# A graph network layer stack: one graph's aggregation of messages moved into the next graph, and a transpose moved ahead of the distances

## The chip, the cores and the metric

The program runs on one core of one Trainium2 chip. The time is the device time of one execution in microseconds (us); the kernel before takes 2127.64 us (median of three runs, 2127.56 to 2128.44). The engines are named as the profile names them: PE (TensorE, matmuls) and PEld (its weight loads), DVE (VectorE), ACT (ScalarE), POOL (GpSimd), SP (SyncE, which only issues transfers here). Each engine works through its own queue in order. A letter q behind an engine (ACTq) is its sequencer, which issues transfers.

## What is computed

For 64 graphs of 256 nodes with 256 channels, in float32, two layers one after the other, each added to its input and normalized:

```python
# layer 0
deg = adj.sum(-1);  dis = deg ** -0.5
norm_adj = dis[:, :, None] * adj * dis[:, None, :]
x1 = layernorm(x + ((norm_adj + alpha * I) @ x) @ W.T + b)
# layer 1
x_conv = relu(bn2(conv17(relu(bn1(conv1(x1))))) + x1)    # along the nodes
s = x1 @ w_se.T + b_se
A = exp(-(sq[:, :, None] + sq[:, None, :] - 2 * s @ s.T)) * adj
msg = relu(x1 @ w_msg.T + b_msg)
x_nmp = A @ msg                                          # the aggregation
out = layernorm(x1 + gru([x_conv, x_nmp], x1))
```

The kernel does the convolution over 17 nodes by a Fourier transform over tiles of nodes, and the GRU's input as one matrix product with a Strassen scheme.

## The kernel before

The 64 graphs go through in four quarters of 16 (`Q`). For a quarter, first each graph's front part runs, layer 0 and what layer 1 can do before the convolution: `layer0` and `layer1` are Python generators, each cut by `yield` into pieces. `graphs` interleaves them: while layer 1 of graph g runs, layer 0 of graph g+2 runs in its gaps. Behind a quarter come the products of the convolution in the frequency domain (`products`, p_k in the profile), the transforms back (`complex_end` and others, many small DVE operations on the tile VM), and the gates (`gru`, p_g) of its graphs. The stages of different quarters overlap: the first 12 graphs of quarter 1 and the first 6 of quarters 2 and 3 (`AHEAD`) run while the quarter before is still in its products and transform; the filter weights (p_u) are made between the graphs of quarter 0.

`layer1` has seven pieces for a graph g:

- 0: x1 is transposed (`x1_transposed`: four PE transposes into p_x1T, and the copies of the two halves into `xn`, one by DVE (L430) and one by ACT (L431)), unless that was done ahead;
- 1: the first convolution and the three columns s (p_conv, L446), their copies by ACT into h and scols, and three small DVE operations (L454 to L457);
- 2: the messages (p_msg, L467, copied by ACT, L470);
- 3: the Fourier transform of h (p_dft, L482, copied by ACT, L487);
- 4: transposes of the columns (p_rows, L495), copied by ACT into dist_l (L497) and by DVE into dist_r (L499);
- 5: the distances (p_dist, L506), Exp by ACT into aT (L507), times the adjacency by DVE (L508);
- 6: the aggregation (p_nmp, L515), its copy by ACT into `xn` (L519) and the transfer of `xn` to memory (L520), issued by ACT.

In the 12 graphs of `ALONE` (16 to 27) x1 of the next graph is transposed at the start of piece 6.

`layer0` of graph g+2 has these parts: degrees by ACT (L356), transposes of adj on PE (p_adjT, L378), copied by ACT (L379), with the diagonal set by DVE (L381), and x scaled by ACT (L391); then p_hT (L399) and its copy by ACT (L404); then p_out (L409) and two DVE operations (L414); then the statistics of the normalization (DVE L325 to L327, a power on POOL, L328); then the normalization (DVE L331, ACT L333) and the transfer of x1.

`PLACES` says behind which piece of layer 1 a part of layer 0, or one of other work (weights, gates), is taken; `STATS` is the piece at which the statistics are taken, and `APPLIED` that at which the normalization of the layer 0 begun a graph earlier is run to its end:

```python
PLACES = (("other",), ("layer0",), (), (), ("layer0",), ("other", "layer0"), ())
STATS, APPLIED = len(PLACES) - 1, 2
```

The kernel's text does not fix each engine's order alone: a scheduler takes instructions by the order of the text and by when it reckons them ready, and hands out buffers from pools. `xn` has two buffers, `msg`, `aT` and `h` one, `adjT` three; the PSUM banks of the front part are a ring of four. `mark` names an operation behind which pieces of the transform's end are put (`paced`, with `RATES`).

Of the kernel before, what the change touches and what calls it, by code (L numbers as in the profile page):

```python
# [14 lines left out]
P = 128  # L15
# [11 lines left out]
def kernel(  # L27
# [27 lines left out]
    nc = tc.nc  # L55
# [4 lines left out]
    NCH = N // P  # L60
    DCH = D // P
# [20 lines left out]
    def bank(name):  # L82
        return ps.tile([P, 512], F32, tag="bank", name=name)
# [7 lines left out]
    def mark(op, gates=0):  # L91
        marks.append((op.ins, gates))
# [11 lines left out]
    def load(g):  # L104
        if g >= B:
            return
        ain[g] = loads.tile([P, NCH, N], F32, name="adj_t")
        nc.sync.dma_start(ain[g], adj[g].rearrange("(c p) m -> p c m", p=P))
        xin[g] = loads.tile([P, NCH, D], F32, name="x_t")
        nc.sync.dma_start(xin[g], x[g].rearrange("(c p) f -> p c f", p=P))  # L110
# [229 lines left out]
    xn_d = [dram.tile([P, 2 * DCH, N], F32, name=f"xn_d{g}") for g in range(B)]  # L340
    XN = {}
    ALONE = set()
# [80 lines left out]
    def x1_transposed(g):  # L423
        x1 = X1.pop(g)
        xn = XN[g] = work.tile([P, 2 * DCH, N], F32, name="xn")
        p = bank("p_x1T").rearrange("p (k n) -> p k n", k=DCH)
        for k in range(DCH):
            for c in range(NCH):
                nc.tensor.transpose(p[:, k, c * P : (c + 1) * P], x1[:, c, k * P : (k + 1) * P], ident)
        nc.vector.tensor_scalar(xn[:, 0], p[:, 0], others_only, unit, op0=ALU.mult, op1=ALU.add)  # L430
        nc.scalar.copy(xn[:, 2 * DCH - 1], p[:, 1])  # L431

    def layer1(g, place):

        if g not in XN:
            x1_transposed(g)
        xn, adjT = XN.pop(g), ADJT.pop(g)
        x1T = xn[:, 0 : 2 * DCH : 2 * DCH - 1]
        yield

        h = work.tile([P, NCH, D], F32, name="h", bufs=1)
        cols = scols.rearrange("p c (q r) -> p c q r", r=32)
        for c in range(NCH):
            p = bank("p_conv1")[:, : D + NSE]
            for k in range(DCH):
                nc.tensor.matmul(  # L446
                    p, x1T[:, k, c * P : (c + 1) * P], wc1[:, k, :], start=k == 0, stop=k == DCH - 1
                )
            nc.scalar.activation(h[:, c, :], p[:, :D], AF.Relu)
            nc.scalar.copy(cols[:, c, :, :NSE], p[:, D:].unsqueeze(1).to_broadcast([P, 4, NSE]))  # L450

        s3 = cols[:, :, 0, :NSE]
        sq3 = small.tile([P, NCH, NSE], F32, name="sq3")
        nc.vector.scalar_tensor_tensor(sq3, s3, -1.0, s3, op0=ALU.mult, op1=ALU.mult)  # L454
        nsq = small.tile([P, NCH], F32, name="nsq")
        nc.vector.tensor_reduce(nsq, sq3, AX.X, ALU.add)
        last = nc.vector.tensor_scalar(  # L457
            cols[:, :, 2:4, NSE], nsq.unsqueeze(2).to_broadcast([P, NCH, 2]), 0.5, None, op0=ALU.mult
        )
        mark(last)  # L460
        mark(last)
        yield
        msg = work.tile([P, NCH, D], F32, name="msg", bufs=1)
        p = bank("p_msg").rearrange("p (c d) -> p c d", c=NCH)
        for c in range(NCH):
            for k in range(DCH):
                nc.tensor.matmul(  # L467
                    p[:, c, :], x1T[:, k, c * P : (c + 1) * P], wmsg[:, k, :], start=k == 0, stop=k == DCH - 1
                )
        mark(nc.scalar.activation(msg, p, AF.Relu))  # L470
        yield


        mid = GT // 2
        if TILES[0] is not V:
            AWAY.append(place)
        for k in range(DCH):
            p = bank("p_dft")

            for c, t0, t1 in ((0, 0, mid + 1), (1, mid - 1, GT)):  # L480
                first = t0 + 1 - c * mid
                nc.tensor.matmul(  # L482
                    p[:, t0 * FL : t1 * FL], h[:, c, k * P : (k + 1) * P],
                    fwd[:, first : first + t1 - t0, :].rearrange("p t f -> p (t f)"),
                    start=c == 0, stop=True, skip_group_check=c == 1,
                )
            nc.scalar.copy(  # L487
                TILES[0][:, :, k, place * GT : (place + 1) * GT],
                p[:, : GT * FL].rearrange("p (t f) -> p f t", f=FL),
            )  # L490

        yield
        p = bank("p_rows")
        for c in range(NCH):
            nc.tensor.transpose(p[:, c * P : (c + 1) * P], scols[:, c, :], ident)  # L495
        dl = work.tile([64, N], F32, name="dist_l", bufs=1)
        nc.scalar.copy(dl, p[0:64, :N])  # L497
        dr = work.tile([64, N], F32, name="dist_r", bufs=1)
        nc.vector.tensor_copy(dr, p[64:P, :N])  # L499
        yield  # L500

        aT = work.tile([P, NCH, 2, P], F32, name="aT", bufs=1)
        for c in range(NCH):
            rows = slice(32 * c, 32 * c + 32)
            p = bank("p_dist")[:, :N]
            nc.tensor.matmul(p, dl[rows, c * P : (c + 1) * P], dr[rows, :], start=True, stop=True)  # L506
            nc.scalar.activation(aT[:, c].rearrange("p n q -> p (n q)"), p, AF.Exp, bias=nsq[:, c : c + 1], scale=2.0)  # L507
        mark(nc.vector.tensor_mul(aT, aT, adjT[:, :, 0:3:2, :]))  # L508
        yield
        if g in ALONE:  # L510
            x1_transposed(g + 1)
        p = bank("p_nmp").rearrange("p (k n) -> p k n", k=DCH)
        for k in range(DCH):
            for mc in range(NCH):
                nc.tensor.matmul(  # L515
                    p[:, k, :], msg[:, mc, k * P : (k + 1) * P], aT[:, mc].rearrange("p n q -> p (n q)"),
                    start=mc == 0, stop=mc == NCH - 1,
                )
        nc.scalar.copy(xn[:, 1 : 1 + DCH], p)  # L519
        nc.scalar.dma_start(xn_d[g], xn)  # L520
        yield

# [410 lines left out]
    def chain(*stages):  # L935
        for stage in stages:
            yield from stage
# [13 lines left out]
    def run(stage):  # L951
        for _ in stage:
            pass
# [14 lines left out]
            yield  # L968


    PLACES = (("other",), ("layer0",), (), (), ("layer0",), ("other", "layer0"), ())
    STATS, APPLIED = len(PLACES) - 1, 2
    ENDS = [iter(())]

    def graphs(first, part, others):


        for i in part:
            load(first + i + 3)
            given = {"layer0": layer0(first + i + 2) if first + i + 2 < B else iter(()), "other": others[i]}  # L980
            for piece, _ in enumerate(layer1(first + i, i)):
                if piece == APPLIED:
                    run(ENDS.pop())
                    ENDS.append(given["layer0"])
                elif piece == STATS:
                    next(given["layer0"], "end")
                yield
                for name in PLACES[piece]:
                    if next(given[name], "end") != "end":
                        yield  # L990
            yield from given["other"]

    with tc.tile_pool(name="setup", bufs=1) as setup:
        load_taps(setup, 0)
# [51 lines left out]
        others = [weights(setup, i, scale2) for i in range(NPARTS)]  # L1046
        others += [take(more_weights, i) for i in (1, 3, 2)]
        run(graphs(0, range(Q), others))
    ustream = ctx.enter_context(tc.tile_pool(name="ustream", bufs=6))

    def open_ahead(graphs):

        scope = ExitStack()
        pool = scope.enter_context(tc.tile_pool(name="ahead", bufs=1))
        return scope, graphs, pool.tile([P, FL, DCH, graphs * GT], F32, name="V2")
# [24 lines left out]
    def copies(V2):  # L1080

        waiting = list(AWAY)
        AWAY.clear()
        TILES[0] = V
        for i in waiting:
            nc.scalar.copy(V[:, :, :, i * GT : (i + 1) * GT], V2[:, :, :, i * GT : (i + 1) * GT])
            yield

    late = nothing()
    for q in range(NQ):  # L1090
        first = (q + 1) * Q
        more = q + 1 < NQ
        end = chain(complex_end(q), copies(V2) if more else iter(()))
# [99 lines left out]
```

## Time and profile before

| | |
|---|---|
| median of 3 runs | 2127.64 us (2127.56 to 2128.44) |
| the profiled execution | 2127.71 us, of which the span 2125.9 us |
| PE busy | 2006.1 us, 94% |
| PEld busy | 1443.2 us, 68% |
| DVE busy | 1474.1 us, 69% |
| ACT busy | 905.3 us, 43% |
| POOL busy | 666.8 us, 31% |
| granted PE clock, mean | 0.988 of full |

The profile is of one execution. Instructions are grouped by line of the kernel, engine, operation and tiles, written out<-in; "idle before" is the time for which the engine had nothing to run just before them, and the arrow names what ended it. A matmul in float32 shows as two records, so four matmuls of the text are eight in the profile. Matmuls are pipelined: their single durations overlap, so that eight records of 379 ns, started one after the other, take 1.73 us.

### The profile page before, as it was taken

The numbers are of one execution on the slowest core, as the hardware profiler recorded it, in microseconds if no ns is written. First come the engines' busy times: TensorE is split into PE (matmuls) and PEld (weight loads), VectorE is DVE, ScalarE is ACT, GpSimd is POOL, SyncE is SP. The second block draws the span as 40 slices with busy tenths as digits, with TensorE's granted clock in tenths as the row PEclk, the third lists the DMA queues.
The fourth block names the chain that finished last, engine by engine and source line by source line (L and its number), as shares of the span: only waits on it lengthen the run. The fifth ranks groups of instructions, "written<-read, shape, count | busy, mean of one in ns | idle before, by whom it ended". The sixth has DMA issues, their size and how long they took to land. (4 is left out here: it accounts for less than half of the span.)

```text
span 2125.9 us, 26260 instructions
## 1 busy us (share of the span) xinstructions
PE 2006.1 (94%) x8157; PEld 1443.2 (68%) x8157; DVE 1474.1 (69%) x3347; ACT 905.3 (43%) x2114; POOL 666.8 (31%) x672
## 2 busy tenths in 40 slices
PE   6999999888999999999999999999999999899997
PEld 5888788766667756667777666667777765555554
DVE  5555567775558788774556888875445889977776
ACT  4666643456432234555553123446554123233333
POOL 3445310121431243223321234323232123344443
PEclk9999999999999999999999999999999999999999
DMA  4766556433437645344335655334323754443331
GB/s 125 230 210 200 192 183 209 154 132 119 122 96 226 194 123 139 114 120 120 94 99 179 201 155 140 118 104 134 96 93 100 243 146 131 111 118 95 93 94 56
DMA packets 305289, 298.05 MB, mean 140 GB/s; under 512 B 84192, under 2 KB 283956, under 8 KB 305150
## 3 DMA queue, kind: packets, MB, share of 16 engines
q1 hardware_dynamic: 245198, 200.37, 32.1%
q10 hardware_dynamic: 44480, 67.39, 8.9%
q0 software_dynamic: 15472, 28.61, 6.0%
q8 instruction: 66, 1.08, 0.2%
q14 instruction: 73, 0.60, 0.1%
HBM read 193.19 MB, written 103.06 MB: 139 GB/s over the span
## 5 line engine op out<-in xcount | busy, mean ns | idle before, releaser
L856 PE MATMUL p_g<-wall,sums 128*128 128x384 f32 x1536 | 537.7, 489 | 11.6 <-DVE G L882 11.6
L856 PE MATMUL p_g<-wall,inputs 128*128 128x384 f32 x1152 | 409.4, 492 | 14.5 <-DVE G L874 14.1
L856 PEld LDWEIGHTS p_g<-wall,sums 128*128 128x128 f32 x1536 | 284.6, 191 | 200.3 <-issue 19.1
L856 PEld LDWEIGHTS p_g<-wall,inputs 128*128 128x128 f32 x1152 | 218.5, 192 | 167.5 <-DVE G L874 23.4
L838 POOL TENSOR_TENSOR sums<-inputs 128x384 f32<-128x384 f32 x128 | 139.9, 1093 | 343.2 <-PE p_g L856 296.9
L369 POOL TENSOR_TENSOR dis<-deg,neg_half 128x2 f32<-128x2 f32 x64 | 48.3, 754 | 475.7 <-DVE deg L367 468.6
L897 ACT ACTIVATE G<-G 128x512 f32<-128x512 f32 x128 | 80.7, 630 | 250.8 <-DVE G L884 148.6
L328 POOL TENSOR_TENSOR ln_rs<-ln_rs,neg_half 128x2 f32<-128x2 f32 x129 | 94.9, 736 | 275.1 <-DVE ln_rs L327 226.7
L541 PE MATMUL p_k<-u,VM 128*128 128x256 f32 x736 | 175.8, 381 | 4.1 <-DMA u<-ud 4.1
L541 PEld LDWEIGHTS p_k<-u,VM 128*128 128x128 f32 x736 | 139.4, 191 | 31.3 <-DMA u<-ud 3.9
L446 PE MATMUL p_conv<-wc,xn 128*128 128x259 f32 x512 | 130.4, 392 | 22.7 <-DVE xn L430 21.5
L399 PE MATMUL p_hT<-adjT,x 128*128 128x256 f32 x512 | 126.7, 391 | 15.6 <-ACT msg L470 8.2
L333 ACT ACTIVATE x_g<-x_g,ln_mr,ln_rs 128x256 f32<-128x256 f32 x128 | 70.0, 593 | 150.3 <-DVE ln_mr L331 148.3
L446 PEld LDWEIGHTS p_conv<-wc,xn 128*128 128x128 f32 x512 | 94.2, 191 | 53.1 <-DVE xn L430 31.1
L508 DVE TENSOR_TENSOR aT<-aT,adjT 128x512 f32<-128x512 f32 x64 | 44.8, 699 | 123.0 <-ACT aT L507 122.8
L409 PE MATMUL p_out<-w,hT 128*128 128x256 f32 x512 | 123.7, 384 | 3.4 <-ACT hT L404 3.0
L482 PE MATMUL p_dft<-fwd,h 128*128 128x240 f32 x512 | 117.4, 372 | 9.2 <-ACT scols L450 8.8
L515 PE MATMUL p_nmp<-aT,msg 128*128 128x256 f32 x512 | 122.6, 383 | 0.7 <-DVE aT L508 0.7
L467 PE MATMUL p_msg<-wmsg,xn 128*128 128x256 f32 x512 | 122.0, 381 | 0.0
L838 POOL TENSOR_TENSOR sums<-inputs,sums 128x384 f32<-128x384 f32 x64 | 70.2, 1097 | 161.3 <-PE p_g L856 160.6
L331 DVE SCALAR_TENSOR_TENSOR ln_mr<-ln_mv,ln_rs 128x2 f32<-128x2 f32 x129 | 47.3, 368 | 101.7 <-POOL ln_rs L328 101.7
L409 PEld LDWEIGHTS p_out<-w,hT 128*128 128x128 f32 x512 | 95.6, 190 | 29.9 <-ACT hT L404 9.9
(160 smaller groups left out, 3642.0 us busy)
## 6 DMA issues: line engine op xcount, KB each, us to landing
u<-ud SPq DMA_DIRECT2D x284, 256.0 KB
xn_d<-xn ACTq DMA_DIRECT2D x64, 512.0 KB
inputs<-xn_d SPq DMA_DIRECT2D x64, 512.0 KB
ud<-u_set POOLq DMA_DIRECT2D x39, 480.0 KB, 6.3
adj_t<-in_adj_dram SPq DMA_DIRECT2D x64, 256.0 KB
x_t<-in_x_dram SPq DMA_DIRECT2D x64, 256.0 KB
x_d<-x ACTq DMA_DIRECT2D x64, 256.0 KB
xc_d<-VM SPq DMA_DIRECT2D x64, 256.0 KB
```

The costliest lines, as they stand in the source:

```text
L328: nc.gpsimd.tensor_tensor(rs[:, : len(chunks)], rs[:, : len(chunks)], neg_half[:, : len(chunks)], op=ALU.pow)
L333: nc.scalar.activation(y[:, c, :], y[:, c, :], AF.Identity, bias=mr[:, c : c + 1], scale=rs[:, c : c + 1])
L399: nc.tensor.matmul(p[:, k, :], x1[:, mc, k * P : (k + 1) * P], adjT[:, mc, 1 - mc : 3 - mc, :].rearrange("p n q -> p (n q)"), start=mc == ...
L409: nc.tensor.matmul(p[:, c, :], hT[:, k, c * P : (c + 1) * P], w0[:, k, :], start=k == 0, stop=k == DCH - 1)
L446: nc.tensor.matmul(p, x1T[:, k, c * P : (c + 1) * P], wc1[:, k, :], start=k == 0, stop=k == DCH - 1)
L467: nc.tensor.matmul(p[:, c, :], x1T[:, k, c * P : (c + 1) * P], wmsg[:, k, :], start=k == 0, stop=k == DCH - 1)
L482: nc.tensor.matmul(p[:, t0 * FL : t1 * FL], h[:, c, k * P : (k + 1) * P], fwd[:, first : first + t1 - t0, :].rearrange("p t f -> p (t f)") ...
L515: nc.tensor.matmul(p[:, k, :], msg[:, mc, k * P : (k + 1) * P], aT[:, mc].rearrange("p n q -> p (n q)"), start=mc == 0, stop=mc == NCH - 1,)
L541: nc.tensor.matmul(p[:, j * D : (j + 1) * D], v[:, k, :], u[:, k, :], start=k == 0, stop=k == DCH - 1)
L838: nc.gpsimd.tensor_tensor(S[i], x, y, op=op)
L856: nc.tensor.matmul(p[:, : 3 * HD] if k == 0 else p[:, HD:], a[:, k], wall[:, b, k].rearrange("p t d -> p (t d)"), start=first and k == 0, ...
L897: nc.scalar.activation(rz, rz, AF.Tanh, scale=0.5)
```

## The change

The aggregation of a graph is taken out of its last piece. The graph only notes what is to be aggregated, in a list `PENDING`; a new function `aggregated` does it in the next graph, as a piece of its own between the adj transposes (which follow piece 1) and the messages. At the end of each run of `graphs` it is called once more for the last graph. The transposes of the next graph's x1, in the graphs of `ALONE`, go to the start of the distances' piece. The pieces are numbered anew: 0 and 1 as before, 2 the aggregation, 3 messages, 4 Fourier transform, 5 rows, 6 distances. The statistics of the layer 0 begun a graph earlier now run behind piece 1 instead of at the end of the graph before, and its normalization behind the messages, as before.

```diff
         mark(last)
         mark(last)
         yield
+        aggregated()
+        yield
         msg = work.tile([P, NCH, D], F32, name="msg", bufs=1)
...
         nc.vector.tensor_copy(dr, p[64:P, :N])
         yield
 
+        if g in ALONE:
+            x1_transposed(g + 1)
         aT = work.tile([P, NCH, 2, P], F32, name="aT", bufs=1)
...
         mark(nc.vector.tensor_mul(aT, aT, adjT[:, :, 0:3:2, :]))
-        yield
-        if g in ALONE:
-            x1_transposed(g + 1)
-        p = bank("p_nmp").rearrange("p (k n) -> p k n", k=DCH)
-        for k in range(DCH):
-            for mc in range(NCH):
-                nc.tensor.matmul(
-                    p[:, k, :], msg[:, mc, k * P : (k + 1) * P], aT[:, mc].rearrange("p n q -> p (n q)"),
-                    start=mc == 0, stop=mc == NCH - 1,
-                )
-        nc.scalar.copy(xn[:, 1 : 1 + DCH], p)
-        nc.scalar.dma_start(xn_d[g], xn)
-        yield
+        PENDING.append((g, xn, msg, aT))
+        yield
+
+    PENDING = []
+
+    def aggregated():
+
+        while PENDING:
+            g, xn, msg, aT = PENDING.pop()
+            p = bank("p_nmp").rearrange("p (k n) -> p k n", k=DCH)
+            for k in range(DCH):
+                for mc in range(NCH):
+                    nc.tensor.matmul(
+                        p[:, k, :], msg[:, mc, k * P : (k + 1) * P], aT[:, mc].rearrange("p n q -> p (n q)"),
+                        start=mc == 0, stop=mc == NCH - 1,
+                    )
+            nc.scalar.copy(xn[:, 1 : 1 + DCH], p)
+            nc.scalar.dma_start(xn_d[g], xn)
...
-    PLACES = (("other",), ("layer0",), (), (), ("layer0",), ("other", "layer0"), ())
-    STATS, APPLIED = len(PLACES) - 1, 2
+    PLACES = (("other",), ("layer0",), (), (), (), ("layer0",), ("other", "layer0"))
+    STATS, APPLIED = 1, 3
     ENDS = [iter(())]
...
             for piece, _ in enumerate(layer1(first + i, i)):
-                if piece == APPLIED:
-                    run(ENDS.pop())
-                    ENDS.append(given["layer0"])
-                elif piece == STATS:
-                    next(given["layer0"], "end")
+                if piece == STATS:
+                    next(ENDS[0], "end")
+                elif piece == APPLIED:
+                    run(ENDS[0])
+                    ENDS[0] = given["layer0"]
                 yield
...
             yield from given["other"]
+        aggregated()
```

## The prediction

> **What bounds the kernel now.** I read the page's head first, then busy times by stretch of the span, then the waits in the stretches that the change touches, and last the timeline of one graph.
>
> ```profile
> span 2125.9 us, 26260 instructions
> PE 2006.1 (94%) x8157; PEld 1443.2 (68%) x8157; DVE 1474.1 (69%) x3347; ACT 905.3 (43%) x2114; POOL 666.8 (31%) x672
> ```
>
> PE is the engine to watch. The next view cuts the span into stages (columns: window, length, busy time and instructions of PE, weight loads, DVE, ACT, POOL, then granted clock).
>
> ```profile
> 240.00:285.00 45.00, 41.01 (x193) 33.85 (x194) 24.42 (x74) 24.90 (x68) 11.24 (x13) 0.96 0.47 150
> ...
> 390.00:516.00 126.00, 109.73 (x536) 87.87 (x537) 95.99 (x273) 69.33 (x188) 24.26 (x26) 1.00 0.37 123
> 516.00:640.00 124.00, 111.00 (x421) 77.21 (x420) 61.48 (x138) 57.70 (x135) 43.58 (x46) 0.94 0.41 111
> ...
> 840.00:1140.00 300.00, 288.17 (x1251) 212.87 (x1250) 184.06 (x478) 159.25 (x400) 90.03 (x92) 1.00 0.36 108
> ...
> 1350.00:1640.00 290.00, 277.36 (x1190) 202.88 (x1189) 170.75 (x447) 149.22 (x374) 84.66 (x86) 0.99 0.34 105
> ```
>
> Graphs run in these windows, in 32-240 (graphs 0-12, filter weights between; PE busy 204.88 of 208) and in 285-390 (104.07 of 105). 640-840, 1140-1350 and all from 1640 on are transform products and gates, which the edit doesn't reorder. Those two full windows have no room. In the five shown PE is idle 4, 16, 13, 12 and 13 us. Who is waited for in 390-516 (sum, times, longest):
>
> ```profile
> DVE aT L508 <- ACT aT L507: 15.5, 8, 2.9
> ...
> DVE ln_mr L331 <- POOL ln_rs L328: 9.9, 9, 1.1
> PE p_conv L446 <- DVE xn L430: 9.6, 7, 3.1
> ```
>
> DVE's 95.99 busy and its waits of 15.5 and 9.9 make 121.4 of 126 us: there DVE, stuck in its own order, is the bound, and PE waits for it. In 840-1140 PE's waits are of another kind:
>
> ```profile
> PE p_hT L399 <- ACT msg L470: 4.5, 4, 2.2
> PE p_conv L446 <- DVE xn L430: 1.8, 3, 1.1
> PE p_rows L495 <- DVE ln_mv L326: 1.6, 1, 1.6
> PE p_rows L495 <- DVE scols L457: 1.3, 2, 0.9
> ```
>
> A row for p_dft behind scols adds 0.7. In 1350-1640 the same rows read 3.7, 1.8, 1.6, 1.3, and 2.0 for p_dft. Last, four rows of the timeline at one graph's end:
>
> ```profile
> 464.79 0.70 PE L506 MATMUL p_dist<-dist_r,dist_l 32*128 32x256 f32 x4
> ...
> 466.39 0.69 DVE L508 TENSOR_TENSOR aT<-aT,adjT 128x512 f32<-128x512 f32 x1 [2.59 <-ACT aT L507]
> ...
> 470.59 0.54 DVE L430 TENSOR_SCALAR xn<-p_x1T,others_only,ident 128x256 f32<-128x256 f32 x1
> ...
> 471.18 1.14 PE L446 MATMUL p_conv<-wc,xn 128*128 128x259 f32 x4 [1.49 <-DVE xn L430]
> ```
>
> PE had been through with the aggregation (p_nmp) for 1.5 us when conv could start, because DVE copied xn late.
>
> **The change part by part.** No instruction is added or removed: the same matmuls, copies and transfers in another order. Every term is an amount of waiting. I read the order from the built programs of both kernels.
>
> *Aggregation later.* Per graph 8 matmul records go from behind p_out to behind the next graph's adj transposes; they take 1.73 us (1414.07 to 1415.81 in the chain). Before, they hid little: in all but 12 graphs p_x1T came after them, so conv waited for xn's copy anyhow. After, 1.73 us more PE work stands between conv and msg, dft, rows and hT, the four that wait for ACT and DVE. ACT also gets the aggregation's copy (0.59) and the issue of xn_d (0.33) there, in front of msg's copy: for waits on ACT's queue the cover is 1.73 - 0.59 = 1.1 (the issue is the sequencer's and lets ACT's next operation start at once in the timeline). In the two long windows: dft 0.7 + 2.0, all single waits under 1.73, go; rows 2.9 + 2.9 go; p_nmp's own wait for aT, 0.3 + 0.4, goes; hT for msg, 8.2 in seven, loses 6.0 (two of 2.2 keep 1.1 each); conv 3.6 loses half, as a p_g group follows p_x1T in most graphs. That is 17.0. But in 840-940 DVE is 81% busy with the transform's end; there PE waits for DVE's work, not for a latency, and more cover doesn't shorten it. I take half: **-8.5**; bounds -17 and 0.
>
> *Window 32-240.* 15.65 us a graph against about 15.0 of matmuls back to back (the 0.6 is p_dist's issue), with eight filter matmuls as filler: **0**. Cover if the filler falls elsewhere: ACT has 77 us idle there, DVE 97.
>
> *Window 240-285.* Conv waits 4.0 in three graphs. After, p_out's two DVE operations (0.48 each, L414) and the copy (0.54) stand between p_out and conv, less 0.44 of p_x1T: about 0.9 each, 2.7. **-1.3**, bounds -4 and +2.
>
> *x1 transposed ahead of the distances (graphs 17-28, window 390-516).* The copy L430 moves out of conv's way: the 9.6 us go. But DVE is the bound, so I follow its loop from one aT to the next: its work to L381 (adjT's diagonal), then hT 1.73, p_x1T 0.44 (new), p_dist, Exp, aT (1.60 from p_dist to aT: 464.79 to 466.39). Gains in each graph: the 1.1 wait for POOL's power goes, as the built order puts 3 to 6 transform operations between L327 and L331; and L430's 0.45 leaves the stretch before L381. Costs: p_x1T's 0.44 in the loop; and in 6 graphs (22 to 27) L430 stands on DVE *ahead* of dist_r's copy, so p_dist waits for p_x1T, L430 and dist_r: 0.2 + 0.45 + 0.43 = 1.1 more. So 1.1 gained in graphs 20 and 21, nothing in six; and graph 20's conv, which waited 3.1, loses some 1.5 to DVE's shorter queue. **-3.5**; bounds -9.6 (all of PE's wait) and +9 (eight graphs at 1.1 if POOL's wait stays).
>
> *xn's two buffers.* Graph g+1's copy now must await the transfer of g-1's xn, issued late in the same graph instead of a graph before. Chain: that transfer held its follower 3.45 us. Counted from p_dist, PE's 2.4 + conv 1.74 + transposes 0.44 + aggregation 1.73, the copy 0.6 and 0.5 of issue make 7.4, with the transfer 10.9; L430 comes near 13.9. **0**, with 3 us to spare; if the cover were gone, the excess would be paid in 12 graphs.
>
> *Queues.* The statistics (L325-L328) move behind conv, their use (L333) behind msg: two small groups on DVE, one 0.74 us power on POOL, two ACT operations and the issue of x1_d later on ACT's queue; x1 is next needed by p_x1T, some 2 us later. On SP and POOL only the order to these shifts; no gate's transfer waits for the xn_d of its last graphs. **0**, bounds -1 and +4.
>
> *Window 516-640.* Conv of graph 29 waits 3.1 at 533, since L430 stands behind the statistics (with the wait for POOL) on DVE; after, it follows L414: about 1.4 is left, -1.7. The granted clock is 0.5 from 536.6 to 540.0: half of 3.4 us could come back, 1.7; I take half of it: **-2.5**, bounds -5 and +2. The 6.1 us at 517, ACT copying twelve graphs' tiles back, stay: those copies wait for DVE's last transform pieces.
>
> A rule of the Trainium skill (TensorE: Matmul & The Clock Gate, "Part 1: The HAM clock gate") says that the clock halves after an idle window of about 3.4 us. This trace has half clock at 591.2 after a wait of only 2.4 us (p_out for hT, at 587), so the row decides; by the rule the 1.7 us would not be there to win and the sum would be 0.8 us less.
>
> New waits from an order nobody ran: +2 (a tenth of the 20 us of waits that I move work across).
>
> Sum: -8.5 - 1.3 - 3.5 - 2.5 + 2 = **-13.8**. The profiled execution took 2127.71 us (span 2125.9), the median is 2127.64: the same. Predicted: **2114 us**.
>
> **The rivals.**
>
> *Moved, not removed.* PE's waits shrink but DVE-bound stretches (390-516, 840-940, 1350-1450) set the pace, and the gates' DVE chains take the rest. For: 121.4 of 126. Against: the later parts, 940-1140 and 1480-1640, where DVE is idle half the time. Only 240-285, 516-640 and a little remain: -4 to +4, 2124 to 2132.
>
> *Slower: L430 ahead of dist_r.* DVE executes in order, so a p_x1T that is late holds dist_r, p_dist, Exp and aT. If POOL's 1.1 stays and x1's normalization comes late too, all 12 graphs pay 0.44 + 1.1 and the 4.5 of waiting that hT and dist_r now cause grows with them: 12 x 1.5 = 18, less 6 won elsewhere: about 2140. It decides once a graph's loop there grows by more than 0.5 us over today's 14.6 (102 us from the aT at 407.8 to that at 509.9, over seven graphs). For: the built order. Against: the removed waits of 9.9.
>
> *Everything goes.* All waits named above: 17 + 4 + 9.6 + 5 = 35.6, about 2092.
>
> **How the numbers follow.** Forecast (2104 to 2122): 0.54; everything or near it (below 2104): 0.12; moved (2123 to 2132): 0.13; slower (above 2132): 0.21. 0.2% of the time, 4.3 us, is about what a measurement tells from no change. Faster 0.66, same 0.12, slower 0.22 (a little of the third case is on the slow side). For 8 in 10 the range leaves out about one in ten at each end: 2101 to 2137; the forecast's own range is 2104 to 2122.
>
> **What would show it.** Right: in 390-516 the rows PE p_conv <- DVE xn and DVE ln_mr <- POOL nearly empty; in the long windows rows <- scols and dft <- scols gone, hT <- msg under 5 for both; no half clock near 537. Wrong: PE p_dist <- DVE dist_r or DVE xn <- PE p_x1T of over 8 us in 390-516, a longer DVE aT <- ACT aT, or L430 waiting for the xn_d transfer. A time above 2132 with those rows makes the second rival true; waits of p_g on DVE G grown by what the graphs lost makes the first.

## The result, and the profile after

The changed kernel takes 2143.82 us (median of four runs, 2137.67 to 2147.18), the kernel before 2128.04 us in the same study (2127.56 to 2129.88). The ratio is 1.0069, 95% interval 1.0045 to 1.0093: slower by 15 us, where 2114 us and a gain were predicted. The profiled execution took 2137.67 us; it is the fastest of the four, and its span is 10.0 us longer than before. So the stages below account for 10 of the 15 us; the three longer runs show a granted clock of 0.982 to 0.986, the profiled one 0.988.

The head of the page after, and busy times by stretch (columns as before):

```profile
span 2135.9 us, 26334 instructions
PE 2004.0 (94%) x8157; PEld 1446.6 (68%) x8157; DVE 1452.0 (68%) x3347; ACT 906.4 (42%) x2114; POOL 664.9 (31%) x672
```

```profile
32.00:240.00 208.00, 194.88 (x936) 158.62 (x936) 101.05 (x240) 121.93 (x315) 86.65 (x82) 0.99 0.60 188
240.00:285.00 45.00, 39.85 (x195) 32.45 (x194) 23.11 (x66) 25.22 (x67) 13.84 (x15) 1.00 0.57 178
390.00:516.00 126.00, 113.27 (x558) 94.74 (x557) 91.10 (x275) 69.26 (x187) 24.94 (x24) 1.00 0.41 137
516.00:640.00 124.00, 107.87 (x426) 76.89 (x425) 58.18 (x148) 63.31 (x146) 42.59 (x45) 0.94 0.41 114
840.00:1140.00 300.00, 286.86 (x1234) 211.46 (x1233) 181.52 (x480) 157.97 (x397) 90.71 (x94) 0.99 0.37 110
1350.00:1640.00 290.00, 277.12 (x1195) 204.85 (x1194) 174.12 (x455) 152.05 (x380) 83.89 (x87) 0.99 0.36 108
```

PE does the same 8157 matmuls. In 32-240 it had been busy 204.88 us of 208 and is now busy 194.88, with 936 matmuls instead of 1014: the stretch that was costed at nothing is where the kernel falls back. Fixed windows show other work once a kernel is shifted, so below I measure stages by work: from the first p_dist of one graph to the first p_dist of another, read from the trace. In every table the time before graph 0's distances is left out; it is 42 to 45 us.

| from graph to graph | before | after |
|---|---|---|
| 0 to 13 (first quarter, filter weights between) | 206.6 | 224.3 |
| 13 to 18 | 118.2 | 119.4 |
| 18 to 27 (the stretch 390-516) | 141.4 | 137.4 |
| 27 to 31 (in 516-640) | 109.3 | 113.4 |
| 31 to 32 (products and gates) | 217.3 | 214.0 |
| 32 to 47 (first long window) | 297.1 | 298.5 |
| 47 to 48 | 210.0 | 207.4 |
| 48 to 63 (second long window) | 294.7 | 293.1 |
| 63 to the end | 489.2 | 486.3 |

17.7 us are lost in the first thirteen graphs, where one came every 15.9 us on the mean and now comes every 17.3; 4.0 are won where the second part of the change acts; 4.1 are lost in the stretch after it; the long windows, which were to bring most of the gain, bring 0.2.

PE's waits of the changed kernel, first in 60-240, where the profile of before lists none at all, then in 840-1140 (sum, times, longest):

```profile
PE p_hT L399 <- ACT msg L472: 9.0, 9, 1.7
```

```profile
PE p_dist L510 <- DVE dist_r L501: 5.1, 3, 2.2
PE p_hT L399 <- ACT msg L472: 3.4, 2, 2.4
PE p_conv L446 <- DVE xn L430: 3.2, 2, 2.1
PE p_rows L497 <- DVE scols L457: 0.9, 2, 0.5
```

In 1350-1640 the same rows read 4.9, 3.4, 3.2 and 0.9. Rows and hT have shrunk and the wait of p_dft is gone, but conv waits longer, and p_dist's wait for dist_r, 0.3 us in each window before, takes 10.0 us in the two. Some of these waits cost more than their length. In these windows the granted clock is 0.5 for 3.4 us four times (from 976.7, 1031.3, 1481.9 and 1536.5), each time right behind a wait of PE of 2.0 to 2.4 us ahead of p_hT or p_dist; before it was so once (from 1430.9). Half of 3.4 us, 1.7, is lost each time, so some 5 us more than before. In 390-516 three rows answer to those shown of before:

```profile
DVE aT L512 <- ACT aT L511: 11.9, 8, 1.7
...
PE p_dist L510 <- DVE dist_r L501: 5.8, 5, 1.2
...
DVE ln_mr L331 <- POOL ln_rs L328: 1.7, 2, 1.1
```

The wait for POOL's power has gone from 9.9 to 1.7, conv's wait for xn (9.6) has no row any more, and what came in its place is p_dist behind dist_r, 5.8 us where 2.3 stood before.

**One graph of the first quarter.** The timeline of the changed kernel, some lines of one graph (start, duration, engine, line; in brackets the idle time before it and the releaser that the profile names):

```profile
157.00 1.22 DVE L331 SCALAR_TENSOR_TENSOR ln_mr<-ln_mv,ln_rs 128x2 f32<-128x2 f32 x1 [1.97 <-POOL ln_rs L328]
...
158.26 0.60 ACT L333 ACTIVATE x<-x,ln_mr,ln_rs 128x256 f32<-128x256 f32 x1 [2.57 <-DVE ln_mr L331]
158.77 0.36 ACT L449 ACTIVATE h<-p_conv 128x256 f32<-128x256 f32 x1
...
159.72 0.37 ACTq L420 DMA_DIRECT2D x_d<-x  x1
...
160.12 0.59 ACT L529 COPY xn<-p_nmp 128x512 f32<-128x512 f32 x1
...
160.74 1.95 ACTq L530 DMA_DIRECT2D xn_d<-xn  x1
...
162.74 0.60 ACT L472 ACTIVATE msg<-p_msg 128x512 f32<-128x512 f32 x1 [2.03 <-PE p_rows L497]
...
163.39 1.35 PE L399 MATMUL p_hT<-adjT,x 128*128 128x256 f32 x5 [1.57 <-ACT msg L472]
```

Two things stand out. L333, the normalization of layer 0, waits 2.57 us at the head of ACT's queue for a DVE operation that waits for POOL; behind it stand h, adjT's copy and the rest. And the issue of xn_d, 1.0 us behind that of x1_d, takes 1.95 us. The copy of msg starts 0.05 us after that issue ends. The bracket names p_rows, which had ended at 161.82; ACT's own sequencer is no releaser to the profile, so its issue has to be read from the ACTq lines. p_hT takes the PSUM bank of p_msg and waits for that copy. Before, the two issues were 5.5 us apart, xn_d's took 0.34 us and msg's copy never waited for it:

```profile
146.12 0.34 ACTq L520 DMA_DIRECT2D xn_d<-xn  x1
...
151.59 0.60 ACT L470 ACTIVATE msg<-p_msg 128x512 f32<-128x512 f32 x1
151.67 0.37 ACTq L420 DMA_DIRECT2D x_d<-x  x1
```

That gave the theories for the runs. Theory 1: the late statistics hold ACT at L333. Theory 2: the issue of xn_d holds msg's copy. Theory 3: the aggregation has no room between p_conv and p_msg, wherever statistics and issue stand.

### The profile page after: what moved, and what is told of

It reads as the page before. It is cut to its first block, busy times and chain, and to the rows that moved or that the text cites. A ratio compares the mean times of both kernels' runs of the same rounds, so it can differ in the third digit from the quotient of the medians.

```text
span 2135.9 us, 26334 instructions
## 1 busy us (share of the span) xinstructions
PE 2004.0 (94%) x8157; PEld 1446.6 (68%) x8157; DVE 1452.0 (68%) x3347; ACT 906.4 (42%) x2114; POOL 664.9 (31%) x672
## 4 chain that ended last, share of the span: by engine, by line
PE 49%; DVE 15%; issue 4%; DMA 3%; POOL 3%; ACT 2%; POOLq 0%; ACTq 0%; SPq 0%; DVEq 0%
PE p_g L865 28%; PE p_k L550 6%; PE p_out L409 3%; PE p_hT L399 2%; PE p_nmp L525 2%; PE p_dft L484 2%; PE p_msg L469 2%; PE p_conv L446 2%; POOL ln_rs L328 1%; PE p_dist L510 1%; DMA inputs<-x_d 1%; DVE VM L601 1%; DVE VM L600 1%; DVE ln_st L325 1%; DMA inputs<-xn_d 1%
## 5 line engine op out<-in xcount | busy, mean ns | idle before, releaser
L550 PEld LDWEIGHTS p_k<-u,VM 128*128 128x128 f32 x736 | 138.9, 190 | 29.6 <-DMA u<-ud 5.1
L399 PEld LDWEIGHTS p_hT<-adjT,x 128*128 128x128 f32 x512 | 95.1, 196 | 46.4 <-ACT msg L472 26.4
L333 ACT ACTIVATE x_g<-x_g,ln_mr,ln_rs 128x256 f32<-128x256 f32 x128 | 70.0, 593 | 132.4 <-DVE ln_mr L331 132.4
L501 DVE COPY dist_r<-p_rows 64x256 f32<-64x256 f32 x64 | 27.3, 426 | 141.2 <-ACT dist_l L499 140.6
```

What stands on the lines that cost most here:

```text
L333: nc.scalar.activation(y[:, c, :], y[:, c, :], AF.Identity, bias=mr[:, c : c + 1], scale=rs[:, c : c + 1])
L399: nc.tensor.matmul(p[:, k, :], x1[:, mc, k * P : (k + 1) * P], adjT[:, mc, 1 - mc : 3 - mc, :].rearrange("p n q -> p (n q)"), start=mc == ...
L550: nc.tensor.matmul(p[:, j * D : (j + 1) * D], v[:, k, :], u[:, k, :], start=k == 0, stop=k == DCH - 1)
```

## The experiments

A ratio is to the kernel before in the same study, with its 95% interval. The studies' medians of the kernel before lie between 2127.97 and 2130.86 us, so a difference between the medians of two studies is good to some 3 us. Stage lengths come from one profiled execution of each: in graphs 32 to 47 the run "The second part alone" executes the same instructions in the same order on every engine as the kernel before, and takes 301.3 us instead of 297.1. A long window is good to some 4 us only; in the first quarter the same two executions agree within 0.2.

### Statistics early

```diff
             for piece, _ in enumerate(layer1(first + i, i)):
-                if piece == STATS:
-                    next(ENDS[0], "end")
-                elif piece == APPLIED:
+                if piece == APPLIED:
...
+            next(given["layer0"], "end")
             yield from given["other"]
```

> Changed kernel, with one thing taken back: layer 0's normalization statistics (L325 to L328) are issued at the end of the graph's own last piece again, as before the change, and not behind the next graph's p_conv. Theory 1 (the statistics come late, POOL's pow L328 stands behind u_set's add and ud's issues, so ACT waits 2.57 us at L333 in 7 of 10 graphs, and h, scols, adjT's, nmp's and msg's copies stand behind it): in 32-240 the graphs come every 15.7 us again instead of 17.2, the distances of graph 13 start near 250 us instead of 266.4, about 2127 us in all. Theory 2 (the issue of xn_d on ACT's queue, 1.0 us behind that of x_d, takes 1.09 us on the mean and holds msg's copy): nothing changes by this, graph 13 at 264 to 267, 2138 to 2144 us. Theory 3 (the aggregation's own copy and PSUM bank between p_conv and p_msg are too much for ACT there, wherever statistics and issues stand): 2138 to 2144 us too.

Measured: 2141.55 us, ratio 1.0054 (1.0035 to 1.0072). ACT's waits at L333 in 60-250 fall from 21.1 us to 2.6, and graphs 0 to 13 still take 224.7 us. Theory 1's number is missed by 14 us. xn_d's issue takes 0.34 us in ten of twelve graphs here and p_hT's wait for msg is down to 1.1 us in 60-240, yet the graphs come no faster: with early statistics the aggregation's new place costs as much without a slow issue. Conv waits 3.5 us for DVE where it had waited for nothing; more shows in the rows of the weight loads, which PE's own rows don't hold: PEld waits 4.8 us at conv for xn (0.7 before), 3.7 at p_msg for scols and 3.4 at p_hT for msg (both without a row before).

### The issue of xn_d behind msg's copy

```diff
             nc.scalar.copy(xn[:, 1 : 1 + DCH], p)
-            nc.scalar.dma_start(xn_d[g], xn)
+            STORED.append((g, xn))
...
-        mark(nc.scalar.activation(msg, p, AF.Relu))
+        done = nc.scalar.activation(msg, p, AF.Relu)
+        mark(done)
+        with tc.issue_after(done.ins):
+            stored()
```

`stored` issues the DMAs of what `STORED` holds.

> Changed kernel, but the DMA of xn_d (L530) is issued from ACT's queue only when msg's copy (L472) is issued, so msg's copy no longer stands behind it. Theory 1: graph 13's distances still start at 262 to 267 us and the time is 2135 to 2144 us. Theory 2: p_hT's waits on msg's copy in 60-240 (19.7 us in the trace of the changed kernel) all but go, graph 13 near 252, about 2128 us. Theory 3: nothing, 2138 to 2144 us.

Measured: 2112.31 us, ratio 0.9916 (0.9901 to 0.9931). Moving one DMA's issue behind one copy takes 31 us off the changed kernel and makes it faster than the kernel before. p_hT's wait for msg, 9.0 us in the changed kernel, has no row in 60-240 any more, but graph 13's distances start at 259 us, where theory 2 had 252. The same place in its timeline:

```profile
158.65 0.37 ACTq L420 DMA_DIRECT2D x_d<-x  x1
159.06 0.58 ACT L532 COPY xn<-p_nmp 128x512 f32<-128x512 f32 x1 [0.44 <-ACT x L333]
159.54 0.60 ACT L472 ACTIVATE msg<-p_msg 128x512 f32<-128x512 f32 x1
159.67 0.90 ACTq L539 DMA_DIRECT2D xn_d<-xn  x1
...
160.20 1.99 PE L399 MATMUL p_hT<-adjT,x 128*128 128x256 f32 x8
```

The issue still takes 0.90 us here, but msg's copy and p_hT no longer stand behind it. The Trainium skill (Perfetto Trace Analysis, "DMA Instruction — HWDGE (DVE, Sync)") says that the profile's span of an issue runs until the sequencer is free for its next instruction; the 1.95 us row above with msg's copy 0.05 us behind it agrees.

But this was not one change. The scheduler, given the new order, also put L333 behind both h copies and adjT's copy, so its 2.57 us wait was gone too; and elsewhere ACT's order moved as well. The runs from "L333 later" on part these.

### Both

> Changed kernel with both edits: statistics at the end of the graph's own last piece, and the DMA of xn_d issued behind msg's copy. If theories 1 and 2 hold together, or either by itself, graph 13's distances start near 250 us and the time is 2120 to 2128 us (the changed kernel gains 3 us elsewhere: 4.0 in 390-516, 3.0 in the long windows, less 4.1 lost in 530-650). Theory 3: still above 2136 us, graph 13 at 260 or later.

Measured: 2161.32 us, ratio 1.0144 (1.0120 to 1.0168): on theory 3's side of 2136, but far above the changed kernel, which no theory explains. Graphs 0 to 13 take 245.5 us. PE's waits in 60-240 and the place in DVE's queue:

```profile
PE p_conv L446 <- DVE ln_mv L326: 18.1, 9, 2.0
```

```profile
142.84 0.74 DVE L325 BATCH_NORM_STATS2 ln_st<-x 128x6 f32<-128x256 f32 x2
143.50 0.17 DVE L326 BATCH_NORM_AGGREGATE ln_mv<-ln_st 128x2 f32<-128x6 f32 x1
143.58 0.51 DVE L430 TENSOR_SCALAR xn<-p_x1T,others_only,ident 128x256 f32<-128x256 f32 x1
...
144.24 2.87 PE L446 MATMUL p_conv<-wc,xn 128*128 128x259 f32 x8 [2.01 <-DVE ln_mv L326]
```

Early statistics stand on DVE ahead of the copy of xn, and conv waits 2 us for it in nine graphs. The clock adds to it: the granted clock is 0.94 of full over graphs 0 to 13 (1.00 before, 0.99 in the changed kernel), with half clock for some 27 us there against 3.4 in the changed kernel, which is worth some 12 of the 21 us between the two. In the kernel before the statistics were early too, but there p_nmp stood between p_out and p_x1T, 1.73 us in which DVE could take them. By this order the aggregation's old place hid something in the first quarter, which the prediction denied (this is argued from the order), and early statistics don't mend the changed kernel.

### The second part alone, on the kernel before

```diff
+        if g in ALONE:
+            x1_transposed(g + 1)
         aT = work.tile([P, NCH, 2, P], F32, name="aT", bufs=1)
...
         yield
-        if g in ALONE:
-            x1_transposed(g + 1)
         p = bank("p_nmp").rearrange("p (k n) -> p k n", k=DCH)
```

> The kernel before with the second part of the change alone: for graphs that stand alone the transposes of x1 (L429 to L431) are issued ahead of the distances, the aggregation and the statistics stay where they were. If this part is what gained in 390-516 (graph 18's to graph 27's distances took 141.4 us before and 137.4 after), that stretch takes 137 to 138 us here, 32-240 is as before (graph 13's distances at 248.7), and the time is about 2124 us. If the aggregation's later place gained it, the stretch takes 141 and the time is 2127 to 2129 us. If dist_r behind xn's copy on DVE costs more than the transposes' wait saved, above 2130 us.

Measured: 2126.41 us, ratio 0.9983 (0.9971 to 0.9994). Graphs 18 to 27 take 138.2 us instead of 141.4, graphs 0 to 13 take 206.8 as before. The second part gains by itself about what it was predicted to. It is no test of L430 ahead of dist_r: in this version that order came about in one graph (26) of the twelve.

### L333 later, the issue where the change put it

```diff
-            nc.scalar.copy(cols[:, c, :, :NSE], p[:, D:].unsqueeze(1).to_broadcast([P, 4, NSE]))
+            HELD[0] = nc.scalar.copy(cols[:, c, :, :NSE], p[:, D:].unsqueeze(1).to_broadcast([P, 4, NSE]))
...
                 elif piece == APPLIED:
-                    run(ENDS[0])
+                    with tc.issue_after(HELD[0].ins):
+                        run(ENDS[0])
```

> Changed kernel, with layer 0's normalization (L333 and the issue of x1_d behind it) held until the second copy of scols has been issued: in 32-240 ACT's queue then reads h, scols, h, scols, L333, adjT, L333 instead of h, scols, L333, h, scols, L333, adjT; the issue of xn_d stays between the aggregation's copy and msg's, as changed. This parts what the last study mixed: with the issue behind msg's copy L333 had also gone behind the h copies, and its 2.57 us wait was gone. Theory 1 (late statistics hold ACT at L333, and h and scols behind it): the graphs in 32-240 come every 16.0 to 16.3 us, as with the issue moved, and the time is 2112 to 2122 us. Theory 2 (the issue of xn_d, up to 2 us, holds msg's copy): they still come every 17 us and the time is 2136 to 2144 us.

Measured: 2126.21 us, ratio 0.9983 (0.9968 to 0.9998). 18 us off the changed kernel, between the two guesses, and not by theory 1: graphs 0 to 13 take 223.5 us as in the changed kernel, and PE's waits there stand (the row below), though L333 now waits mostly 1.7 us instead of 2.57 and behind the h copies:

```profile
PE p_hT L399 <- ACT msg L472: 8.4, 9, 1.8
```

PE's order is the same instruction for instruction; ACT's differs, and DVE's in a few places. The profiled execution is the fastest of its ten, 8.5 us below their median. The gain lies in 27 to 31 (106.6 us instead of 113.4), in the long windows (292.3 and 287.4 instead of 298.5 and 293.1) and in the last stage (481.2 instead of 486.3). What differs there is the place of a gate's operation. The changed kernel, in the first long window:

```profile
1025.58 0.48 ACT L489 COPY VM<-p_dft 128x384 f32<-128x384 f32 x1 [0.21 <-PE p_dft L484]
...
1027.50 1.31 POOL L822 TENSOR_TENSOR inputs<-inputs 128x512 f32<-128x512 f32 x1
1028.85 0.51 ACT L825 ACTIVATE inputs<-inputs,bn_bias 128x256 f32<-128x256 f32 x1 [2.79 <-POOL inputs L822]
...
1029.26 0.46 ACT L489 COPY VM<-p_dft 128x384 f32<-128x384 f32 x1
1029.62 0.36 ACT L499 COPY dist_l<-p_rows 64x256 f32<-64x256 f32 x1
...
1030.02 0.43 DVE L501 COPY dist_r<-p_rows 64x256 f32<-64x256 f32 x1 [5.85 <-ACT dist_l L499]
...
1030.50 0.70 PE L510 MATMUL p_dist<-dist_r,dist_l 32*128 32x256 f32 x4 [2.20 <-DVE dist_r L501]
```

L825, which waits for POOL and a transfer, stands between the two copies of p_dft. ACT waits 2.79 us there, dist_l and dist_r come late, and p_dist with them. Near 600 us the same order costs 4.1 us at once. With L333 later, the scheduler puts L825 behind dist_l:

```profile
1020.45 1.01 ACT L489 COPY VM<-p_dft 128x384 f32<-128x384 f32 x2
1021.36 0.36 ACT L499 COPY dist_l<-p_rows 64x256 f32<-64x256 f32 x1
...
1022.76 0.91 ACT L825 ACTIVATE inputs<-inputs,bn_bias 128x256 f32<-128x256 f32 x2 [1.04 <-POOL inputs L822]
1022.82 0.30 PEld L510 LDWEIGHTS p_dist<-dist_r,dist_l 32*128 32x128 f32 x4 [0.33 <-issue]
```

p_dist's wait for dist_r in 840-1140 falls from 5.1 to 1.0, and the half clock at that place is gone. In the built orders L825 stands between two copies of p_dft five times in the changed kernel, with the statistics early and with xn_d on SP, and never in the other versions. In the three, 27 to 31 takes 112.3 to 113.4 us, in all others that have the later aggregation 106.6 to 110.3; p_dist's wait for dist_r is 3.6 to 6.4 us in each long window in the three and at most 1.4 in the others. L825 was not moved by itself in any run, so that it is the cause is argued from this split.

### The other issue moved

```diff
-        nc.scalar.dma_start(x1_d[g // Q][g % Q].rearrange("(c p) d -> p c d", p=P), x1)
+        if MSG:
+            with tc.issue_after(MSG[-1]):
+                nc.scalar.dma_start(x1_d[g // Q][g % Q].rearrange("(c p) d -> p c d", p=P), x1)
+        else:
+            nc.scalar.dma_start(x1_d[g // Q][g % Q].rearrange("(c p) d -> p c d", p=P), x1)
...
+        MSG.append(done.ins)
```

`MSG` holds the copies of msg issued so far; the first graphs, without one, issue at once.

> Changed kernel, with the DMA of x1_d (L420) issued behind msg's copy and that of xn_d (L530) where the change put it, so that no other issue of ACT stands 1 us ahead of L530. If L530's 0.34 to 2.04 us come from the nearness of the two issues on one queue, it takes 0.34 us each time and the time is about 2130 us. If they come from the backlog of the loads and stores that SP and POOL have issued in the 5 us before, L530 still takes 0.8 to 1.5 us on the mean in 60-240 and the time stays at 2138 to 2144 us.

Measured: 2117.48 us, ratio 0.9939 (0.9917 to 0.9962), lower than both guesses; L825 moved here too. Graphs 0 to 13 take 215.6 us, and each of xn_d's twelve issues in 60-250 takes 0.34 us:

```profile
160.63 0.34 ACTq L537 DMA_DIRECT2D xn_d<-xn  x1
161.01 0.60 ACT L477 ACTIVATE msg<-p_msg 128x512 f32<-128x512 f32 x1 [0.41 <-PE p_dft L491]
161.04 0.67 ACTq L423 DMA_DIRECT2D x_d<-x  x1
```

Now it is x1_d's issue, the second of the two, that takes long: 0.37 to 1.96 us, 0.83 on the mean, with half the bytes. L333 waits its 2.57 us in most graphs here, and most come every 16.0 us all the same (16.2 with the issue late, where L333 doesn't wait). In graphs 0 to 13 this run is one change: PE, DVE, POOL and SP execute the same order as in the changed kernel, and ACT too but for x1_d's issue. So the two issues' standing together cost 8.7 us there, of the two the second is the slow one, and theory 1 is out for the first quarter.

### xn_d from SP's queue

```diff
-            nc.scalar.dma_start(xn_d[g], xn)
+            nc.sync.dma_start(xn_d[g], xn)
```

> Changed kernel, with the DMA of xn_d issued from SP's queue, everything else in ACT's queue in the order of the changed kernel (L333 ahead of the second h copy, with its 2.57 us wait). If the 0.34 to 2.04 us of L530 are the price of ACT's own queue having sent x1_d 1.0 us before, SP's issue takes 0.3 to 0.5 us, p_hT's waits on msg go and the graphs in 32-240 come every 16.0 us, as with x1_d's issue moved instead. If they are the backlog of all queues together, SP's issue takes 0.8 to 2 us too, with ACT free of it all the same. Either way graph 13's distances start at 257 to 261 us, unless SP, standing at the semaphore of the aggregation's copy, sends adj_t's load behind it too late: then p_adjT waits for adj_t, and graph 13 is at 264 or later.

Measured: 2127.30 us, ratio 0.9996 (0.9980 to 1.0013): 16.5 us off the changed kernel.

```profile
173.77 0.37 ACTq L420 DMA_DIRECT2D x_d<-x  x1
...
174.94 0.60 ACT L472 ACTIVATE msg<-p_msg 128x512 f32<-128x512 f32 x1
175.07 0.36 SPq L530 DMA_DIRECT2D xn_d<-xn  x1
```

SP's issue takes 0.34 to 0.50 us (mean of eleven: 0.37), at the same distance from x1_d's. So the 0.34 to 2.04 us (mean of eleven: 1.03) of the changed kernel belong to ACT's own queue, not to a backlog of all queues. Graphs 0 to 13 take 214.2 us, 10.1 less than in the changed kernel (the order of DVE, POOL and SP moved a little too); 27 to 31 takes 112.3, with L825 still between the copies. Another 6.2 us are won in graphs 18 to 27, at another place (below). The Trainium skill (DMA: Bandwidth & Descriptors, "Issuing engines are not separate DMA queues") says that issuing from several engines saves only the time of the issue on the sequencer, usually small beside the transfer. Here that time was worth some 9 to 10 us of the first quarter (8.7 with x1_d's issue moved, 10.1 here), because msg's copy stood behind it.

Against the changed kernel's median xn_d on SP gives 16.5 us, L333 later 17.6, and the issue late, which has both changes of order, 31.5. Each taken against the kernel before of its own study it is 16.5, 19.8 and 34.3.

### The first quarter as before

On top of the issue behind msg's copy; for the first 16 graphs the aggregation and the statistics go back to the graph's own end, for all others they stay where the change has them:

```diff
-                if piece == STATS:
+                if piece == STATS and not first + i - 1 in range(Q):
                     next(ENDS[0], "end")
...
+            if first + i < Q:
+                aggregated()
+                stored()
+                next(given["layer0"], "end")
+                yield
             yield from given["other"]
```

> The version with xn_d issued behind msg's copy (2112.3 us), and in the first quarter's 16 graphs the aggregation, its copy and issue and the statistics at the graph's own end, as in the kernel before. In 32-240 that version still loses 10.6 us to the kernel before (graph 13's distances at 259.1 less 41.9, against 248.7 less 42.1). If that is the price of the aggregation between p_conv and p_msg where the filter already covers everything, graph 13's distances start at 248 to 250 us and the time is 2101 to 2104 us. If what is won there is given back where the loads or the throttle set the pace, 2108 to 2113 us.

Measured: 2103.48 us, ratio 0.9878 (0.9853 to 0.9902). Graphs 0 to 13 take 206.5 us again, and PE has no wait in 60-240. The 10.6 us that the late issue left are the price of the aggregation's new place and the statistics' together, in the quarter where filter matmuls cover all else; no run with the late issue took back the aggregation alone. Early statistics with the aggregation left in its new place ("Both") only cost time, so the place of the aggregation, theory 3, is the likelier of the two.

### The second part taken back

```diff
-        if g in ALONE:
-            x1_transposed(g + 1)
         aT = work.tile([P, NCH, 2, P], F32, name="aT", bufs=1)
...
+        if g in ALONE:
+            x1_transposed(g + 1)
         PENDING.append((g, xn, msg, aT))
```

On the version with the issue late:

> The version with xn_d issued behind msg's copy, and the change's second part undone: in 390-516 the transposes of x1 stand behind the distances' product again. By itself the second part shortened that stretch by 3.2 us (141.4 to 138.2, graphs 18 to 27). If the later aggregation gives the same cover there, the stretch takes 138 to 139 us and the time is 2112 us; if only the second part does, it takes 141 to 142 us and the time is 2115 to 2116 us.

And on the version with the first quarter as before:

> The fastest version so far (2103.5 us: xn_d issued behind msg's copy, the first quarter's graphs aggregated at their own end), and the change's second part undone. With the issue moved the second part was worth nothing (2112.3 with it, 2113.1 without), so 2102 to 2106 us here. If it is worth the 3.2 us that it gave on the kernel before, 2106 to 2108 us.

Measured: 2113.09 us, ratio 0.9922 (0.9896 to 0.9948), against 2112.31 with the second part; and 2102.59 us, ratio 0.9876 (0.9856 to 0.9896), against 2103.48. No difference in time either way. Graphs 18 to 27 take 135.3 us without the second part in both, and 138.8 and 138.9 with it. Beside the later aggregation it is not needed, and in that stretch it costs some 3.5 us, which the totals don't show. The traces show where: with the second part L430 stands on DVE ahead of dist_r's copy in graphs 20 to 27 in both versions, and p_dist waits 1.15 us for dist_r in each of the eight.

| from graph to graph | before | after | L333 later | xn_d on SP | issue late | first quarter as before |
|---|---|---|---|---|---|---|
| 0 to 13 | 206.6 | 224.3 | 223.5 | 214.2 | 217.2 | 206.5 |
| 18 to 27 | 141.4 | 137.4 | 137.5 | 131.3 | 138.8 | 138.9 |
| 27 to 31 | 109.3 | 113.4 | 106.6 | 112.3 | 107.4 | 107.4 |
| 32 to 47 | 297.1 | 298.5 | 292.3 | 298.2 | 293.9 | 293.5 |
| 48 to 63 | 294.7 | 293.1 | 287.4 | 295.9 | 287.8 | 286.2 |

The 131.3 us for graphs 18 to 27 with xn_d on SP fit the same row: L430 stands ahead of dist_r in graphs 22 to 27 in the changed kernel, with p_dist waiting 1.15 us in each, and in graph 24 alone with xn_d on SP; p_dist's wait in 390-516 is 1.7 us there instead of 5.8. No run moved L430 by itself.

## Why the prediction was wrong

- **Window 32-240: 0.** This step failed, with +17.7. It counted idle time (77 us on ACT) as cover. The wait isn't for a share of ACT but for one copy, and what stood in front of that copy decided. With the issue out of its way 7.1 us (issue late) to 10.1 us (xn_d on SP) come back; the rest came back only with the aggregation and the statistics at the graph's own end. What exactly holds the graphs up by that rest stays open.
- **Aggregation later, the sentence on ACT's queue.** That "the issue is the sequencer's and lets ACT's next operation start at once" was read from 0.34 us rows. With xn_d's issue behind x1_d's it took up to 2.04 us, and msg's copy stood behind it. Moving that issue to SP gave back 10.1 us of the first quarter and 16.5 in all. From graph 13 on the sentence held: there xn_d's issue took at most 0.44 us in the changed kernel.
- **Queues: 0, bounds -1 and +4.** It followed the statistics and x1_d's issue to their readers, but not the two issues to their new distance on ACT's queue: 5.5 us before, 1.0 after. That the two had become neighbours stood in the built order.
- **New waits: +2.** The term was there and too small. With L825 between the copies of p_dft p_dist waited 10.0 us in the long windows and 4.1 us once near 600, and the half clock after such waits came on top.
- **Aggregation later: -8.5.** Cover was gained, the changed kernel hides it: -0.2 there (+1.4 and -1.6). In the versions with L825 out of the way the two long windows gain 12.1 (L333 later: 4.8 + 7.3), 10.1 (issue late) and 12.1 us (first quarter as before), near the forecast and inside its bounds; over all seven such versions it is 6.4 to 14.1. With L333 later PE's waits there fall from 11.3 and 12.1 to 8.9 and 9.1 us, 5.4 in all, so part of the 12.1 is the spread of single executions. conv's share was wrong: its wait grew from 1.8 and 1.8 to 3.2 and 3.2, where half of it was to go.
- **x1 ahead of the distances: -3.5.** The size was right: -4.0 in the changed kernel, -3.2 by this part alone. The cost that was named was right too: p_dist waits 1.15 us in each of the graphs 22 to 27, where L430 stands ahead of dist_r. The attribution wasn't: the later aggregation alone (issue late, second part taken back) gives -6.1 in that stretch.
- **Window 240-285: -1.3, bounds -4 and +2.** From graph 13 to 16 it took 58.7 us instead of 56.9, +1.8, near the upper bound.
- **Window 516-640: -2.5.** +4.1, the size of p_dist's one wait from 597.8 to 601.9, before which L825 stands in front of p_dft's second copy; with L825 behind dist_l it is -1.9 (issue late) and -2.7 (L333 later). The working read the wait at 533 as 3.1 us and the one at 587 as 2.4; the rows of PE show 2.92 and 2.23. In the changed kernel half clock came behind waits of 2.0 to 2.4 us too, so deciding by the row was right. The half clock near 537 stayed: the granted clock is 0.66 in 535-540 before, 0.64 there and 0.68 in 540-545 after.
- **xn's two buffers: 0.** Right; no wait of L430 for a transfer appears.
- **The rivals.** The time fell on the side of "Slower", above 2132, but for another reason. Its place, 390-516, became faster, and its row, p_dist behind dist_r, reads 5.8 us there where over 8 would have shown it. That sign did come, 8.1 and 9.2 us, in the issue late and the first quarter as before, both faster than the kernel before, so it is no sign of a slow kernel. The slow rival was looked for where the profile showed waits, while the loss arose in the one stretch that had none.

With the one issue moved, the same change takes 2112.3 us, against the 2114 that were forecast. Part of that agreement is luck: the first quarter is still 10.6 us slower there, and other stages gain more than was said.

## What to carry to other kernels

When work moves on an in-order queue, look at what it lands next to, its DMA issues above all: an issue right behind another of the same engine can hold that engine's next copy, for up to 2 us here, and another engine's queue, or a place behind the copy, cost less. A stretch without waits is not a stretch with room: work that fills gaps in stages that wait may be left where it was in the stage that doesn't. And where a scheduler decides the order, one moved instruction moves others, so compare the built order of every engine before calling an experiment one change.

## What was not expected of the hardware

- In the first quarter an issue on ACT's queue takes 0.34 to 0.38 us when the queue's last issue was 5 to 11 us ago (kernel before), and 0.34 to 2.04 us (mean 1.03) when it was 1.0 us ago (changed kernel); the second one is slow whichever tensor it carries, and SP's issue at the same moment isn't. Distance is not all. In the long windows of the changed kernel xn_d's issue stands 0.5 to 1.3 us behind x1_d's ten times and takes 0.34 to 0.42 us; what the first quarter adds is open. And there too: with the statistics early the two issues are also 1.0 us apart, and there nine of eleven took 0.34 us and two 1.12 and 1.18. In that version POOL's last issue (ud) lies 4.2 us before xn_d's in these graphs and 2.6 in most of the changed kernel; but at 3.9 and 4.1 us the changed kernel has two of 1.02, and with the issue late 0.34 to 0.90 us go with 3.8, so this is hardly the whole reason.
- DVE's L331 on 128x2 takes 1.22 to 1.23 us instead of 0.16 when POOL's add on 128x512 (L392) starts just before it. It is not what slowed the first quarter: with x1_d late it is still 1.23 in eight of eleven, and most graphs come every 16.0 us.
